# Two graph layers on one core: closings in five spread steps, edge-sum blocks begun one selection later, and the MLP's first layer for 512 nodes inside the last attention pass

## The chip, the cores and the metric

The kernel runs on one core of a Trainium2 chip. The metric is the device time of one launch in microseconds (us), as the median of several runs; the time before is 2317.66 us (three runs, 2315.4 to 2319.2). All profiles are of one execution each.

## The reference, cut to what matters

There are 3327 nodes of 1024 features and a sparse, weighted, symmetric adjacency matrix. Layer 0 is a quantised graph convolution. Layer 1, which the change is about, is graph attention with 8 heads of 64 features, and an MLP behind it:

```python
h = relu(layernorm(x))
Wh = einsum('nf,hfd->hnd', h, W)
e_src = einsum('hnd,hd->hn', Wh, a1)
e_dst = einsum('hnd,hd->hn', Wh, a2)
e = leaky_relu(e_src[:, :, None] + e_dst[:, None, :], 0.2)
e = where(adj[None] > 0, e, -9e15)
att = softmax(e, axis=-1)
enc = elu(einsum('hnm,hmd->hnd', att, Wh)).transpose(1, 0, 2).reshape(n, 512)
out = relu(enc @ W1.T + b1)        # 512 -> 256
out = relu(out @ W2.T + b2)        # 256 -> 256
out = relu(out @ W3.T + b3)        # 256 -> 512
x = x + out @ W4.T + b4            # 512 -> 1024
```

## The kernel before, in words

Nodes are padded to 26 tiles of 128 (`T = 26`). Layer 0 ends with the features, the scores and the mask of the adjacency matrix in DRAM. The change is in what follows, and in one line on the order in which the buffers of layer 0 are laid out.

**Attention as selections.** The exponential of a leaky rectifier has two branches: exp(s + d) if s + d > 0, and exp(0.2 (s + d)) if not. Each factors into a part of the source and a part of the destination. So a head needs, for each node, the sum over neighbours of `f` on the first branch and on the second. The kernel makes a 0/1 *selection* on VectorE (L617): neighbour, and s > -d. TensorE multiplies it with the features (L626, `acc<-sel,f`), with columns for both branches, each split into two parts, 260 columns in all. The second branch's sum over the selected neighbours is then subtracted from its sum over all neighbours. That last sum doesn't depend on the selection; it is the *edge sum* (L534, `mps<-dw,mf`), a product of the mask, cast to floats by ScalarE (L533), with the second branch's features of two heads.

**Passes and units.** The 26 tiles of target nodes fall in two halves of 13, and each half in 7 + 6 tiles. A *pass* is one head for 7 or 6 target tiles: 26 selections of 7 x 128 or 6 x 128 elements, each followed by 7 or 6 matmuls. A *unit* is four passes: two heads, one half. There are 8 units and 32 passes, 832 selections. The loop over passes is `for i, (c, g, e, si) in enumerate(attends)`; in the text, n counts selections from 0 to 831, and j within a pass. Selections have four buffers (pool `sel`), accumulators seven PSUM banks.

**Edge sums between the selections.** A unit has 13 edge blocks of 26 matmuls. The generator `all_edges` yields after each matmul, and `edge_steps(n)` says how many are to be done by selection n: unit 0's until n = LATE, then each later unit's within 104 selections. In the first six selections of a unit's span none are due, in the next 13 two each. A block accumulates in the only bank of the pool `s3_m`. At its end ScalarE copies the bank to `part` (L538), and after 7 and 13 blocks VectorE adds the two parts into `md` (L542).

**Closing.** After a pass ScalarE copies the accumulators to `xs` (L638), VectorE adds the parts (L641, `su`), and `close` does the rest: ScalarE scales the first branch (L567), VectorE subtracts and adds (L568, L569) and takes the reciprocal of the denominator (L571), ScalarE normalises and forms the exponential (L574 to L577), VectorE finishes (L579), and GpSimd's queue writes the result to `enc_d` (L580). For a pass with `e == 0` the closing is issued at selection 24 of the next pass, for one with `e == 1` at the end of its own pass.

**MLP.** Seven groups of 4 tiles (the last of 2). Each group is transposed (L719), goes through three layers (`dense`, L683, with the rectification on ScalarE at L690) and the output layer (L731), is added to `x1` and the bias on VectorE (L727, L741) and written out. Loads are issued on SP (L698, L700 for nodes; L669 for weights).

The order on each engine is made by a scheduler from the program; an instruction given to `tc.keep_in_program_order` stays where the program has it.

Of the kernel before, what the change touches and what calls it, by code (L numbers as in the profile page):

```python
# [8 lines left out]
F32 = mybir.dt.float32  # L9
# [50 lines left out]
def two_layer_kernel(  # L60
# [103 lines left out]
    def large(stack, name, shape, dtype=F32):  # L164
        pool = tc.tile_pool(name=name, bufs=1, side="right", reuse_waits="tile")
        return stack.enter_context(pool).tile(shape, dtype, name=name)

    with tc.tile_pool(name="wh", bufs=1, reuse_waits="tile") as whp, tc.tile_pool(
# [57 lines left out]
        with tc.tile_pool(name="s1", bufs=2, reuse_waits="tile") as s1, tc.tile_pool(  # L226
# [94 lines left out]
            w_life.close()  # L321
            supp = ExitStack()

            s_int = [large(supp, f"s_int{t}", [P, F], F32R) for t in range(T)]

            whead = whp.tile([P, KF, EMB], F32, name="whead")
            a1_t = whp.tile([P, EMB], F32, name="a1_t")
# [144 lines left out]
    STEPS = 4 * T  # L472
    EDGE = 13 * T
    START = T - 2
    LATE = 2 * T + START
    with ExitStack() as wide, tc.tile_pool(name="f1", bufs=1, reuse_waits="tile") as f1p, tc.tile_pool(
        name="sel", bufs=4, reuse_waits="tile"
    ) as selp, tc.tile_pool(name="srow", bufs=2, reuse_waits="tile") as srowp, tc.tile_pool(name="mf", bufs=2, reuse_waits="tile") as mfp, tc.tile_pool(
        name="md", bufs=2, reuse_waits="tile"
# [1 line left out]
        name="s3_acc", bufs=7, space=PSUM, reuse_waits="tile"  # L481
    ) as acc_ps, tc.tile_pool(name="s3_m", bufs=1, space=PSUM, reuse_waits="tile") as m_ps:
        f_odd = f1p.tile([P, T, HW], F32R, name="f_odd")
        masks = [large(wide, "mask0", [P, 7, T, P], U8)]
        f_even = large(wide, "f_even", [P, T, HW], F32R)
        dw = large(wide, "dw", [P, T, HW], F32R)
        masks.append(large(wide, "mask1", [P, 6, T, P], U8))
        xs = large(wide, "xs", [P, 7, 2, 2 * HC])

        def load_features(dst, ap, h, pieces):  # L490
            for js in pieces:
# [17 lines left out]
        def all_edges():  # L509

            for u, (c, g) in enumerate(units):
# [13 lines left out]
                for i in range(len(blocks)):  # L525
                    mask = upcoming
                    if i + 1 < len(blocks):
                        upcoming = mask_of(i + 1)
                    ps = m_ps.tile([P, HW], F32, tag="mps", name="mps")
                    for j in range(T):  # L530
                        if j % TH == 0:
                            mf = mfp.tile([P, TH, P], F32R, tag="mf", name="mf")
                            nc.scalar.copy(mf, mask[:, j : j + TH, :])  # L533
                        nc.tensor.matmul(ps, mf[:, j % TH, :], dw[:, j, :], start=(j == 0), stop=(j == T - 1))  # L534
                        if j == T - 1:
                            if i in (0, 7):
                                part = mdp.tile([P, 7, 2, 2 * HC], F32, tag="part", name="part", bufs=1)
                            nc.scalar.copy(part[:, i % 7], ps.rearrange("p (q c) -> p q c", q=2))  # L538
                            if i in (6, 12):
                                r = slice(i - i % 7, i + 1)  # L540
                                n = i % 7 + 1
                                nc.vector.tensor_tensor(md[:, r], part[:, :n, 0], part[:, :n, 1], ALU.add)  # L542
                        yield

        def edge_steps(n):

            if n < START:
                return min(n, START)
            if n < LATE:
                return START + (EDGE - START) * (n - START) // (LATE - START)  # L550
            u, m = divmod(n - LATE, STEPS)
            if u == len(units) - 1:
                return EDGE * len(units)

            first = min(T, max(0, (m - 6) * 2))
            return EDGE * (u + 1) + first + (EDGE - T) * max(0, m - 19) // (STEPS - 19)

        mds = []
        late = None
        edges = all_edges()  # L560
        done = 0
        def close(h, sub, su, md):

            nb = len(sub)
            up, dn = su[:, :nb, 0], su[:, :nb, 1]
            for b, t in enumerate(sub):
                nc.scalar.activation(up[:, b], up[:, b], AF.Copy, scale=ratio[:, t, h : h + 1])  # L567
            nc.vector.tensor_tensor(dn, md, dn, ALU.subtract)  # L568
            nc.vector.tensor_tensor(up, up, dn, ALU.add)  # L569
            rs = small.tile([P, 7, 1], F32, tag="rs", name="rs")  # L570
            nc.vector.reciprocal(rs[:, :nb], up[:, :, HD:])  # L571
            ht = s3.tile([P, 7, HD], F32, tag="ht3", name="ht3", bufs=2)
            for b in range(nb):
                nc.scalar.activation(ht[:, b], up[:, b, :HD], AF.Copy, scale=rs[:, b])  # L574
            ex = s3.tile([P, 7, HD], F32, tag="ex", name="ex")
            nc.scalar.activation(ex[:, :nb], ht[:, :nb], AF.Relu, scale=-1.0)
            nc.scalar.activation(ex[:, :nb], ex[:, :nb], AF.Exp, scale=-1.0)  # L577

            nc.vector.scalar_tensor_tensor(ht[:, :nb], ex[:, :nb], -1.0, ht[:, :nb], ALU.add, ALU.max)  # L579
            nc.gpsimd.dma_start(  # L580
                enc_d[sub[0] * P : (sub[-1] + 1) * P, h * HD : (h + 1) * HD].rearrange(
                    "(b p) d -> p b d", p=P
                ),
                ht[:, :nb],
            )

        old, young = PARTS[:3], [range(20, 24), range(24, 25), range(25, 26)]
        load_mask(0, SUBS[0])
# [6 lines left out]
            load_features(dw, dsum_d, 0, [js])  # L595
        load_features(f_odd, feat_d, 1, old + young)
        for i, (c, g, e, si) in enumerate(attends):
            h = 2 * g + e
            sub, mask = halves[c][si], masks[si]
            nb = len(sub)  # L600
# [3 lines left out]
            for j in range(T):  # L604
# [24 lines left out]
                while done < edge_steps(n + 1):  # L629
                    next(edges)  # L630
                    done += 1
                if j == START and late is not None:
                    late()
                    late = None
            srow = srow_next
            md = mds[i // 4][:, sub[0] - 13 * c : sub[0] - 13 * c + nb, e * HC : (e + 1) * HC]
            for b in range(nb):
                nc.scalar.copy(xs[:, b], accs[b].rearrange("p (q c) -> p q c", q=2))  # L638
            su = s3.tile([P, 7, 2, HC], F32, tag="su", name="su")
            s2d = su.rearrange("p b q c -> p b (q c)")  # L640
            nc.vector.tensor_tensor(s2d[:, :nb], xs[:, :nb, 0], xs[:, :nb, 1], ALU.add)  # L641
            late = lambda h=h, sub=sub, su=su, md=md: close(h, sub, su, md)
            if e == 1:
                late()
                late = None

    mlp = ctx.enter_context(ExitStack())
    row = large(mlp, "row", [P, 7 * NP // 4])  # L650
    enc_x1 = [large(mlp, "nodes0", [P, T * HW])]
    weights = large(mlp, "weights", [P, T * HW])
    enc_x1.append(large(mlp, "nodes1", [P, 4 * (EMB + F)]))
    enc_x1 = [
        (
            n[:, : 4 * EMB].rearrange("p (q e) -> p q e", q=4),
            n[:, 4 * EMB : 4 * (EMB + F)].rearrange("p (q e) -> p q e", q=4),
        )
        for n in enc_x1
    ]  # L660
    bb4 = row[:, :F]
    bb1, bb2, bb3 = (row[:, F + 4 * i : F + 4 * i + 4] for i in range(3))
    w_at = 0

    def weight(ap, k, m):
        nonlocal w_at
        wt = weights[:, w_at : w_at + k * m].rearrange("p (k m) -> p k m", k=k)
        w_at += k * m
        nc.sync.dma_start(wt, ap.rearrange("(k p) m -> p k m", p=P))  # L669
        return wt  # L670

    w1, w2, w3 = weight(w1t, EMB // P, D1), weight(w2t, D1 // P, D2), weight(w3t, D2 // P, D3)
    with tc.tile_pool(name="s4", bufs=2, reuse_waits="tile") as s4, tc.tile_pool(
        name="s4_ps", bufs=4, space=PSUM, reuse_waits="tile"
    ) as ps_p, tc.tile_pool(name="s4_o", bufs=2, space=PSUM, reuse_waits="tile") as o_ps:

        def dense(xt, k_n, wt, bt, m_n, cols, tag):

# [13 lines left out]
                )  # L692
            return yt

        def load_nodes(i, t0):
            enc, x1 = enc_x1[i]
            for q, t in enumerate(range(t0, min(t0 + 4, T))):
                nc.sync.dma_start(enc[:, q, :], enc_d[t * P : (t + 1) * P, :])  # L698
            for q, t in enumerate(range(t0, min(t0 + 4, T))):
                nc.sync.dma_start(x1[:, q, :], x1_d[t * P : (t + 1) * P, :])  # L700

        load_nodes(0, 0)
        w4 = weight(w4t, D3 // P, F)
        nc.sync.dma_start(bb4, b4.partition_broadcast(P))
        with nc.allow_non_contiguous_dma(reason="biases of a few hundred elements"):
            for bb, b in ((bb1, b1), (bb2, b2), (bb3, b3)):
                m = b.shape[0] // P
                nc.sync.dma_start(bb[:, :m], b.rearrange("(m p) -> p m", p=P))
        for g, t0 in enumerate(range(0, T, 4)):
            tiles = range(t0, min(t0 + 4, T))  # L710
            cols = len(tiles) * P
            enc, x1 = enc_x1[g % 2]
            if t0 + 4 < T:
                load_nodes((g + 1) % 2, t0 + 4)
            enct = s4.tile([P, EMB // P, 512], F32, name="enct")
            for k in range(EMB // P):
                tp = ps_p.tile([P, 512], F32, tag="ps", name="tp4")
                for q, t in enumerate(tiles):
                    nc.tensor.transpose(  # L719
                        tp[:, q * P : (q + 1) * P], enc[:, q, k * P : (k + 1) * P], ident  # L720
                    )
                nc.scalar.copy(enct[:, k, :cols], tp[:, :cols])
            h1 = dense(enct, EMB // P, w1, bb1, D1 // P, cols, "h1")
            h2 = dense(h1, D1 // P, w2, bb2, D2 // P, cols, "h2")
            h3 = dense(h2, D2 // P, w3, bb3, D3 // P, cols, "h3")
            for q, t in enumerate(tiles):
# [60 lines left out]
```

## Time and profile before

| what | before |
|---|---|
| median of three runs | 2317.66 us |
| the profiled execution's own time | 2316.48 us |
| its span, first to last instruction | 2314.7 us |
| mean granted TensorE clock | 0.995 |
| first attention matmul to the last one | 988.5 to 2003.3 us |
| MLP, first transpose to the end | 2003.8 to 2314.7 us |

The engines are TensorE (PE, with its weight loads as PEld), VectorE (DVE), ScalarE (ACT), GpSimd (POOL) and SyncE (SP, which only issues transfers). A line of the timeline holds the start, the length, the engine, the line of the kernel, the operation and its tiles; in brackets stands how long the engine was idle just before, and what it then waited for. A line of the waits holds the total in us, how many times, and the longest. [...]

### The profile page before, as it was taken

What the parts mean: (1) busy time and instruction counts of PE and PEld (TensorE: products, weight loads), DVE (VectorE), ACT (ScalarE), POOL (GpSimd) and SP (SyncE); (2) the same over time, 40 slices, a digit from 0 to 9 for tenths busy, and PEclk for the clock granted to TensorE, in tenths of its full rate; (3) what the DMA queues carried; (4) which work ended last, traced back from release to release, by engine and by line L of the source; (5) the groups of instructions that cost most, each with busy time, mean ns of one, the idle gap of its engine ahead of it and who ended that gap; (6) DMA issues with size and microseconds to landing.
All of it is one profiled execution on the core that took longest, in us unless ns stands there. A gap on an engine that the chain in (4) does not pass through costs nothing. (4 is left out here: it accounts for less than half of the span.)

```text
span 2314.7 us, 32013 instructions
## 1 busy us (share of the span) xinstructions
PE 2252.5 (97%) x12884; PEld 1788.4 (77%) x12896; DVE 1567.1 (68%) x2090; ACT 1003.0 (43%) x1654; POOL 119.0 (5%) x173
## 2 busy tenths in 40 slices
PE   4999999999999999899999999999999999999999
PEld 2467777777777777589999999999999999644444
DVE  7845555555555555487999999999999999812211
ACT  4743334333333333346555555555555555311110
POOL 0000011011110110100000000000000000000000
PEclk9999999999999999999999999999999999999999
DMA  6324444444444444743324241545242332433311
GB/s 231 128 90 149 147 159 135 154 157 149 152 152 137 165 155 144 278 145 112 112 73 147 80 146 45 197 156 162 79 143 83 117 105 71 152 109 114 131 56 55
DMA packets 150302, 304.94 MB, mean 132 GB/s; under 512 B 10173, under 2 KB 91021, under 8 KB 150153
## 3 DMA queue, kind: packets, MB, share of 16 engines
q1 hardware_dynamic: 130248, 229.72, 29.7%
q0 software_dynamic: 19904, 73.17, 9.7%
q8 instruction: 101, 1.65, 0.3%
q14 instruction: 49, 0.39, 0.1%
HBM read 216.07 MB, written 86.79 MB: 131 GB/s over the span
## 5 line engine op out<-in xcount | busy, mean ns | idle before, releaser
L617 DVE SCALAR_TENSOR_TENSOR sel<-srow,ndst,mask 128x896 fp32r<-128x896 f32 (+1 forms) x832 | 869.6, 1082 | 61.2 <-PE acc L626 49.7
L534 PE MATMUL mps<-dw,mf 128*128 128x260 f32 x2704 | 462.7, 284 | 0.0
L443 PE MATMUL mm<-s_int,hi 128*128 128x512 f32 x1352 | 433.0, 399 | 0.0
L443 PE MATMUL mm<-s_int,lo 128*128 128x512 f32 x1352 | 421.6, 391 | 0.0
L626 PE MATMUL acc<-f_even,sel 128*128 128x260 f32 x2704 | 403.9, 284 | 1.4 <-DVE sel L617 1.3
L533 ACT CAST mf<-mask 128x1664 fp32r<-128x1664 uint8 x208 | 330.0, 1588 | 167.1 <-PE mps L534 129.3
L626 PE MATMUL acc<-f_odd,sel 128*128 128x260 f32 x2704 | 393.9, 285 | 6.9 <-DVE sel L617 6.8
L534 PEld LDWEIGHTS mps<-dw,mf 128*128 128x128 f32 x2704 | 379.8, 188 | 9.3 <-ACT part L538 8.4
L626 PEld LDWEIGHTS acc<-f_odd,sel 128*128 128x128 f32 x2704 | 352.6, 188 | 15.9 <-DVE sel L617 12.2
L626 PEld LDWEIGHTS acc<-f_even,sel 128*128 128x128 f32 x2704 | 356.7, 188 | 5.9 <-DVE sel L617 2.8
L443 PEld LDWEIGHTS mm<-s_int,lo 128*128 128x128 f32 x1352 | 253.8, 188 | 57.6 <-issue 5.7
L443 PEld LDWEIGHTS mm<-s_int,hi 128*128 128x128 f32 x1352 | 252.1, 188 | 55.6 <-issue 5.7
L184 DVE TENSOR_SCALAR mk<-at 128x896 uint8<-128x896 f32 x104 | 61.7, 593 | 262.6 <-DMA at<-in_adj_t 261.9
L179 ACT CAST hi<-at 128x896 fp32r<-128x896 f32 x104 | 92.7, 891 | 328.7 <-PE mm L443 294.8
L384 PE MATMUL whm<-whead,ht 128*128 128x512 f32 x416 | 186.9, 602 | 0.8 <-ACT ht L381 0.8
L731 PE MATMUL o<-weights,h 128*128 128x512 f32 x416 | 179.7, 592 | 0.0
L731 PEld LDWEIGHTS o<-weights,h 128*128 128x128 f32 x416 | 79.0, 190 | 99.1 <-issue 99.0
L384 PEld LDWEIGHTS whm<-whead,ht 128*128 128x128 f32 x416 | 77.5, 191 | 98.1 <-issue 87.7
L183 DVE TENSOR_TENSOR lo<-at,hi 128x896 fp32r<-128x896 f32 x104 | 106.6, 1025 | 51.3 <-ACT hi L179 39.9
L538 ACT COPY part<-mps 128x260 f32<-128x260 f32 x104 | 39.1, 376 | 216.3 <-PE mps L534 216.3
L741 DVE TENSOR_TENSOR yo<-o,nodes 128x1024 f32<-128x1024 f32 (+1 forms) x27 | 31.8, 1182 | 146.0 <-PE o L731 146.0
L332 PE MATMUL mm<-w_int,xqt 128*128 128x512 bf16 x404 | 98.3, 393 | 9.5 <-DVE w_int L319 7.3
(128 smaller groups left out, 1566.9 us busy)
## 6 DMA issues: line engine op xcount, KB each, us to landing
feat_d<-fw POOLq DMA_DIRECT2D x26, 1040.0 KB, 5.3
f_even<-feat_d SPq DMA_DIRECT2D x7, 3380.0 KB, 12.8
f_odd<-feat_d SPq DMA_DIRECT2D x7, 3380.0 KB, 13.6
at<-in_adj_t SPq DMA_DIRECT2D x52, 448.0 KB, 3.9
at<-in_adj_t SPq DMA_DIRECT2D x52, 384.0 KB, 3.1
mask<-mask_d SPq DMA_DIRECT2D x39, 416.0 KB, 7.7
dw<-dsum_d SPq DMA_DIRECT2D x16, 910.0 KB, 5.1
dsum_d<-dw POOLq DMA_DIRECT2D x26, 520.0 KB, 6.5
```

The lines of the kernel that those rows point to most:

```text
L179: ins = nc.scalar.copy(hi, at)
L183: nc.vector.tensor_tensor(lo, at, hi.bitcast(F32), ALU.subtract)
L184: nc.vector.tensor_scalar(mk[:, r], at, 0.0, None, ALU.is_gt)
L332: nc.tensor.matmul(mm[:, c * 512 : (c + 1) * 512], xqts[t][:, k, :], w_int[:, k, c * 512 : (c + 1) * 512], start=(k == 0), stop=(k == KF - 1),
L384: nc.tensor.matmul(whm, ht[:, k, :], whead[:, k, :], start=(k == 0), stop=(k == KF - 1))
L443: nc.tensor.matmul(mm[:, c * 512 : (c + 1) * 512], which[:, q, :], s_int[j][:, c * 512 : (c + 1) * 512], start=(j == 0 and which is hi), s ...
L533: nc.scalar.copy(mf, mask[:, j : j + TH, :])
L534: nc.tensor.matmul(ps, mf[:, j % TH, :], dw[:, j, :], start=(j == 0), stop=(j == T - 1))
L538: nc.scalar.copy(part[:, i % 7], ps.rearrange("p (q c) -> p q c", q=2))
L617: nc.vector.scalar_tensor_tensor(sel[:, :nb], srow[:, :nb], ndst[:, j, h : h + 1], mask[:, :, j, :], ALU.is_gt, ALU.mult,)
L626: nc.tensor.matmul(accs[b], sel[:, b, :], f[:, j, :], start=(j == 0), stop=(j == T - 1))
L731: nc.tensor.matmul(ps[:, c * 512 : (c + 1) * 512], h3[:, k, q * P : (q + 1) * P], w4[:, k, c * 512 : (c + 1) * 512], start=(k == 0), stop= ...
```

## The change

Four things, and what they need.

- **Closings.** `close` becomes a generator of five steps. Its VectorE instructions are kept in program order. At every third selection (every second, if two closings are open) one step is issued, if the edge sums that the next step needs are done.
- **Edge blocks.** After the last matmul of a block the loop stops until the next selection. `LATE` becomes 62 instead of 76, and the last unit's edges are spread over 118 selections instead of 104.
- **First layer.** Transposes and first layer of the MLP for the first 512 nodes are issued within the last pass, through the bank of the edge sums, one step at selections 6 to 9 and then at each second one. The MLP's buffers lie in those of the features, the edge features and the first mask, which are given up before the last pass.
- **Layout.** Buffers on the right side are laid out in another order, and the buffers of layer 0 in reverse, so that the same ones overlap.

```diff
-            s_int = [large(supp, f"s_int{t}", [P, F], F32R) for t in range(T)]
+            s_int = [large(supp, f"s_int{t}", [P, F], F32R) for t in reversed(range(T))][::-1]
...
-    LATE = 2 * T + START
+    LATE = 62
+    LAST = 14
+    xs = large(wide, "xs", [P, 7, 2, 2 * HC])
+    masks = [None, large(wide, "mask1", [P, 6, T, P], U8)]
+    dw = large(early, "dw", [P, T, HW], F32R)
+    f_even = large(early, "f_even", [P, T, HW], F32R)
+    masks[0] = large(early, "mask0", [P, 7, T, P], U8)
...
-            u, m = divmod(n - LATE, STEPS)
-            if u == len(units) - 1:
-                return EDGE * len(units)
+            u = min((n - LATE) // STEPS, len(units) - 2)
+            m = n - LATE - STEPS * u
+            span = STEPS + (LAST if u == len(units) - 2 else 0)
             first = min(T, max(0, (m - 6) * 2))
-            return EDGE * (u + 1) + first + (EDGE - T) * max(0, m - 19) // (STEPS - 19)
+            rest = (EDGE - T) * max(0, m - 19) // (span - 19)
+            return EDGE * (u + 1) + first + min(rest, EDGE - T)
...
-        def close(h, sub, su, md):
+        def close(i):
...
+            sums = EDGE * (i // 4) + (EDGE if si else 7 * T)
+            yield 0
+            su = s3.tile([P, 7, 2, HC], F32, tag="su", name="su")
+            pin(nc.vector.tensor_tensor(s2d[:, :nb], xs[:, :nb, 0], xs[:, :nb, 1], ALU.add))
             for b, t in enumerate(sub):
                 nc.scalar.activation(up[:, b], up[:, b], AF.Copy, scale=ratio[:, t, h : h + 1])
-            nc.vector.tensor_tensor(dn, md, dn, ALU.subtract)
-            nc.vector.tensor_tensor(up, up, dn, ALU.add)
+            yield sums
+            pin(nc.vector.tensor_tensor(dn, md, dn, ALU.subtract))
+            yield 0
+            pin(nc.vector.tensor_tensor(up, up, dn, ALU.add))
+            yield 0
-            nc.vector.reciprocal(rs[:, :nb], up[:, :, HD:])
+            pin(nc.vector.reciprocal(rs[:, :nb], up[:, :, HD:]))
...
+            yield 0
+            pin(nc.vector.scalar_tensor_tensor(ht[:, :nb], ex[:, :nb], -1.0, ht[:, :nb], ALU.add, ALU.max))
...
+        def close_more():
+            if closing and closing[0][1] <= done:
+                gen = closing[0][0]
+                need = next(gen, None)
+                closing[0] = gen, need
+                if need is None:
+                    closing.pop(0)
...
+            if i == len(attends) - 1:
+                early.close()
...
+                load_nodes(0, 0)
+                w1 = weight(w1t, EMB // P, D1)
...
+                def first_layer():
+                    for k in range(EMB // P):
+                        tp = m_ps.tile([P, 512], F32, tag="mps", name="tp0")
+                        for q in range(4):
+                            nc.tensor.transpose(
+                                tp[:, q * P : (q + 1) * P],
+                                enc_x1[0][0][:, q, k * P : (k + 1) * P],
+                                ident,
+                            )
+                        nc.scalar.copy(enct0[:, k], tp)
+                        yield
+                    for m in range(D1 // P):
+                        ps = m_ps.tile([P, 512], F32, tag="mps", name="h0_ps")
+                        for k in range(EMB // P):
+                            nc.tensor.matmul(ps, w1[:, k, m * P : (m + 1) * P], enct0[:, k],
+                                start=(k == 0), stop=(k == EMB // P - 1))
+                            if k == EMB // P - 1:
+                                nc.scalar.activation(h1_0[:, m], ps, AF.Relu, bias=bb1[:, m : m + 1])
+                            yield
...
                 while done < edge_steps(n + 1):
                     next(edges)
                     done += 1
-                if j == START and late is not None:
-                    late()
-                    late = None
+                    if done % T == 0:
+                        break
+                if i == len(attends) - 1 and FRONT <= j and (j < FRONT + 4 or j % 2 == 0):
+                    next(first_group, None)
+                pace = 2 if len(closing) > 1 else 3
+                if j % pace == pace - 1:
+                    close_more()
...
-            late = lambda h=h, sub=sub, su=su, md=md: close(h, sub, su, md)
-            if e == 1:
-                late()
-                late = None
+            gen = close(i)
+            closing.append((gen, next(gen)))
+        while closing:
+            close_more()
...
+        enc_x1.append(nodes("nodes1"))
...
+            if g == 0:
+                h1 = h1_0
```

## The prediction

> **What bounds the kernel now.** First the page's busy line, then busy time by stretch (one full unit of attention, the last pass, the MLP):
>
> ```profile
> PE 2252.5 (97%) x12884; PEld 1788.4 (77%) x12896; DVE 1567.1 (68%) x2090; ACT 1003.0 (43%) x1654; POOL 119.0 (5%) x173
> core 0: us, PE busy (x) PEld busy (x) DVE busy (x) ACT busy (x) POOL busy (x), PEclk, DMA share, GB/s
> 1235.00:1360.00 125.00, 124.49 (x1012) 122.25 (x1011) 119.12 (x127) 68.59 (x124) 3.64 (x4) 1.00 0.33 105
> 1990.00:2006.00 16.00, 14.91 (x99) 12.46 (x99) 15.99 (x18) 2.68 (x8) 0.97 (x1) 1.00 0.06 15
> 2006.00:2315.00 309.00, 303.11 (x788) 140.46 (x786) 61.72 (x55) 53.09 (x97) 0.85 (x1) 0.99 0.29 101
> ```
>
> TensorE bounds nearly everything; only the last pass belongs to VectorE (15.99 of 16.00). A unit (one pair of heads, one half of the nodes) is 4 passes = 104 selections: 104 x 6.5 attention matmuls + 13 x 26 edge matmuls = 1014. How long is one? Within runs the timeline spaces starts by 0.120 us: attention runs start at 1300.32 and 1301.40 with 6 + 3 matmuls between, 1.08 / 9. So 1014 x 0.120 = 121.7 us is the floor. The unit's real period is 125.5 us: TensorE's longest wait for a selection recurs at 1107.61 and, two units on, at 1358.68. So 3.8 us per unit are lost. Where? Idle before the weight loads in the same unit, then one edge block's end, then that long wait:
>
> ```profile
> PEld mps L534 <- ACT part L538: 1.0, 5, 0.2
> PEld acc L626 <- DVE sel L617: 0.9, 2, 0.7
> PEld acc L626 <- ACT xs L638: 0.2, 1, 0.2
> ...
> 1302.12 0.52 PE L534 MATMUL mps<-dw,mf 128*128 128x260 f32 x3
> 1302.47 0.64 PE L626 MATMUL acc<-f_even,sel 128*128 128x260 f32 x4
> 1302.67 0.38 ACT L538 COPY part<-mps 128x260 f32<-128x260 f32 x1 [2.08 <-PE mps L534]
> 1303.10 0.19 PEld L534 LDWEIGHTS mps<-dw,mf 128*128 128x128 f32 x1 [0.20 <-ACT part L538]
> 1303.10 0.39 PE L534 MATMUL mps<-dw,mf 128*128 128x260 f32 x1
> ...
> 1358.68 0.99 PE L626 MATMUL acc<-f_odd,sel 128*128 128x260 f32 x6 [0.48 <-DVE sel L617]
> ```
>
> An edge block's last matmul starts at 1302.36; the next block can start 0.74 us later, after the copy out of the only bank. Four attention matmuls lie between: 5 x 0.12 = 0.60. So 0.14 is lost, and as the weights were not loaded ahead, the next start comes 0.105 later than usual: 0.25 per block end. A unit has five of these and a 0.2: 1.45 us. Waits for a selection (at 1357.2 and 1358.7, with refills) cost 1.05; the handing over of banks at pass ends some 0.75; the rest is scattered.
>
> VectorE's slack, and the end of attention:
>
> ```profile
> DVE sel L617 <- PE acc L626: 4.5, 24, 0.3
> DVE su L641 <- ACT xs L638: 0.5, 2, 0.4
> ...
> 1990.42 12.16 DVE L617 SCALAR_TENSOR_TENSOR sel<-srow,ndst,mask 128x768 fp32r<-128x768 f32 x13
> ...
> 2006.25 7.30 PE L683 MATMUL h_ps<-enct,weights 128*128 128x512 f32 x16
> 2013.39 10.84 PE L683 MATMUL h_ps<-h,weights 128*128 128x512 f32 x24
> 2024.06 10.46 PE L731 MATMUL o<-weights,h 128*128 128x512 f32 x24
> ```
>
> Back to back a 6-block selection costs 12.16 / 13 = 0.935 us (alone it shows 1.02), a 7-block one about 1.06. Embedded small operations cost less than they show too: start to next start 0.48 to 0.55 for the 0.56 to 0.64 us adds, 0.11 for the reciprocal. VectorE's floor per unit is 52 x (0.935 + 1.06) + 10.4 for four closings + 1.9 for the edge sums = 116 us.
>
> **Which measure of headroom.** By TensorE's busy row, 124.49 of 125, nothing is left: 0.5 us per unit, 4 in all. The Trainium skill (Perfetto Trace Analysis, Identifying the Most-Contended Engine) says that matmul busy time is no measure of headroom and the weight loads' share is: 122.25 of 125, so 2.75 per unit, 22 in all, near my spacing. The same section takes occupancy as fair for VectorE, and that speaks against this change: 119.1 of 125 leaves 5.9 us, and the pinned waits below would use it up, for a gain of nothing here. The back-to-back spacing says 116 and 9.5 us of slack. I take the trace's spacing.
>
> **The change, part by part.** Against the profiled execution: span 2314.7, time 2316.48, 1.2 below the median.
>
> *Edge blocks one selection later.* In the built order, six or seven attention matmuls now lie between every two blocks: the next start comes 7 x 0.12 = 0.84 or 0.96 us on, against 0.74 needed. Cover is thin with six (0.10), so I leave 0.2 of the 1.45: gain 1.25 per unit. If ScalarE is in a 1.59 us mask cast when a block ends, up to 1.6 comes back, once; the built order puts the copies ahead of the next casts.
>
> *Closings spread, their VectorE steps pinned.* Operations and durations are the same; where two closings stood together within 7 selections at the end of a unit (568, 569, 571, 641, 579, 568, 569, 571: 3.8 us in six selections), now one step follows every third selection. The stretch short of edge matmuls after a unit's last block is now five 7-block selections plus about 11 with one to six edge matmuls each. There VectorE needs 16 x 1.06 + 2.4 (edge sum and four steps) = 19.4 us, TensorE 16 x 0.84 + 27 x 0.12 = 16.7; four buffers give a lead of some 2.5. The wait falls from 1.05 to 0.3: gain 0.75 per unit.
>
> *New waits.* The first add of a closing stands after 3 or 4 selections of the new pass and waits for six or seven accumulator copies (0.25 to 0.3 each, about 1.8 us after the pass's last matmul). A full four-selection lead makes VectorE wait 0.8 (after 4) or 2 (after 3); before it waited 0.5 per unit. Queued behind are the selections, and TensorE behind those. The last step stands 4 selections (4.3 us at least) after the reciprocal; its ScalarE chain is 1.78 + 0.58 + 0.58 = 3.0, or 4.6 with a cast between. Bounds: 0 and 3.6 us per closing; nearest to the 0.4 and 0.2 us waits shown, but with a fuller lead, I take 1.4, or 5.6 per unit. 116 + 5.6 = 121.6, under TensorE's new 123.5: hidden.
>
> *LATE 62 for 76.* Unit 0's 314 edge matmuls fall on 38 selections rather than 52, the last unit's on 14 more; TensorE's sum stays. In the last unit TensorE has 118 x 0.78 + 338 x 0.12 = 132.6 us, VectorE 116 x 118 / 104 = 131.6: cost 0, up to 4 if the waits show there. The edge features' loads (first piece issued 1340.61, landed 4.8 later) move along on SP; the piece is free over 6 us before the block ends and needed five selections after it. At the change of halves seven mask loads move past the per-block ones: 0, at most 5 us once.
>
> *Reversed buffers.* The same memory comes free in the same order: 0.
>
> Attention: 2.0 x 8 units = 16 us.
>
> *First layer in the last pass.* Before: 16 transposes (1.75) and 8 matmuls (each recorded as two: 17.54 / 20 = 0.877 each, 7.0) after the last pass. In it TensorE has 156 x 0.12 = 18.7 us of work in about 29, so 8.75 more fits; but late matmuls crowd: the last 8 selections give VectorE 8.1 us and TensorE 8 x 0.72 + 4 x 0.877 = 9.3, so the pass ends 1.2 later. Its loads go early on SP as before (nodes landed 1945.85 to 1954.79; first weights 5.3 us after their issue).
>
> What is late next: the last closing. In the built order four 1.22 us bias adds stand before its first add on VectorE, and its 6 scalings (1.55) and 6 normalisings (1.54) stand on ScalarE each before a rectification (0.69) of the second layer. From the last attention matmul's end T: adds done about T+3, first add T+4, scalings T+5.6, rectification T+6.3, normalisings, second rectification T+8.6; seven of the third layer's eight matmuls follow: T+14.7. Before, that point was 2024.06 with T = 2003.5; now 2003.5 + 1.2 + 14.7 = 2019.4: gain 4.7 us, not 8.75. Without the queueing 8.3; with double 1.
>
> The second group's node loads now wait for the last closing's write, about 10 us later than 2005.87; the first output add is queued behind them on VectorE, but TensorE has two output banks, 13.7 us: hidden by some 8.
>
> Sum: 16 + 4.7 = 20.7. 2316.5 - 20.7 = 2295.8; against the median, 2297.
>
> **Rivals.** (1) VectorE becomes the bound through its pinned waits: a unit stays at 125, attention gains 0 to 5, the tail 5: 2308 to 2313. For: the lead grows as TensorE stalls less. Against: 9.5 us of slack. (2) Slower: the same waits at their upper end, 3.6 us in each closing: 116 + 14.4 = 130.4 per unit, 8 x 4.9 - 4.7 = +34, 2352. It decides from 2.5 us per closing. (3) Only bank handovers and scatter stay (unit 122.4) and the tail's rectifications are not queued: 25 + 8 = 33, 2285. (4) The first layer does not hide, the last pass grows by what is saved: 16 alone, 2302.
>
> **Numbers.** Forecast with (4): 0.70; (3) 0.12; (1) 0.11; (2) 0.07. The forecast's own range is 2290 to 2304; 2286 to 2309 leaves out two in ten, half of (3), most of (1) and (2). What a measurement can tell from no change is about 0.2%, 4.6 us: faster 0.88 (some of (1) falls within), same 0.05, slower 0.07.
>
> **What would show it.** Unit period 123.5 (125.5 before); waits of edge weight loads for the part copy near 0 (8.4 us over attention); waits of VectorE's first closing add for the accumulator copies up, from 3.6 to 20 to 40 us; TensorE idle before the third layer's second matmul by 2 to 4 us; output matmuls of group 0 starting about 15 us after the last attention matmul. Wrong if TensorE's waits for selections exceed 15 us over attention, or the last pass grows by over 3.

## The result, and the profile after

The changed kernel takes 2293.2 us in the median (2292.1 to 2294.8, 4 runs), the kernel before 2317.9 beside it. The ratio is 0.9895, 95% interval 0.9878 to 0.9912. The forecast was 2297.0 within 2286 to 2309. The profiled execution spans 2291.7 us, against 2314.7.

The busy line of the page, then busy time by stretch: one full unit (123 us now) and the last pass. The columns are TensorE, weight loads, VectorE, ScalarE, GpSimd.

```profile
PE 2233.5 (97%) x12896; PEld 1785.0 (78%) x12896; DVE 1559.1 (68%) x2090; ACT 998.2 (44%) x1654; POOL 119.3 (5%) x173
1235.00:1358.00 123.00, 123.00 (x1014) 122.37 (x1013) 118.53 (x127) 68.42 (x125) 3.64 (x4) 1.00 0.34 106
1959.00:1989.00 30.00, 29.32 (x196) 24.51 (x194) 29.98 (x37) 12.24 (x37) 1.81 (x2) 1.00 0.54 181
```

The busy line hardly differs; the stretches do. TensorE's 1014 matmuls of a unit now fill 123.00 of 123.00 us. In the last pass TensorE and VectorE are both nearly full, where before VectorE alone was:

```profile
1976.00:2004.00 28.00, 24.50 (x161) 20.55 (x160) 28.00 (x36) 9.95 (x35) 1.81 (x2) 1.00 0.41 138
```

The waits over the whole of attention, before and then after: TensorE, its weight loads, VectorE.

```profile
PE acc L626 <- DVE sel L617: 8.0, 13, 2.0
PEld acc L626 <- DVE sel L617: 15.0, 36, 2.2
PEld mps L534 <- ACT part L538: 8.4, 43, 0.2
DVE sel L617 <- PE acc L626: 49.7, 208, 0.7
DVE su L641 <- ACT xs L638: 3.6, 14, 0.4
```

```profile
PE acc L738 <- DVE sel L729: 1.1, 1, 1.1
PEld acc L738 <- DVE sel L729: 4.3, 16, 1.3
PEld mps L539 <- ACT part L543: 0.3, 1, 0.3
DVE sel L729 <- PE acc L738: 41.2, 142, 1.7
DVE su L580 <- ACT xs L753: 2.8, 8, 0.4
```

The copy out of the edge bank stops one weight load instead of 43, and selections hold up the weight loads less than a third as long. The last row is the one that the prediction wanted at 20 to 40: it fell.

By the starts of the attention matmuls, where the span's 23.0 us went:

| | before | after | gain, us |
|---|---|---|---|
| first attention matmul | 988.5 | 989.4 | -0.9 |
| attention without its last pass | 987.6 | 970.3 | 17.3 |
| last pass, first to last matmul | 27.2 | 29.2 | -2.0 |
| last attention matmul to first output matmul | 20.7 | 12.1 | 8.6 |

The later start can't be put down to the change: in the eleven kernels here that leave attention's start alone it lies between 986.1 and 990.5.

The unit's period fell from 125.53 to 123.20 us. A matmul of 260 columns is recorded with 0.28 us, but the next one starts 0.120 us after it. Summing over a unit what each start lies beyond that spacing gives 3.84 us lost before, 1.52 now. Sorted by place and by what the weight load waited for, as the mean of units 2 to 6:

| lost per unit, us | before | after |
|---|---|---|
| block ends (part copy) | 1.42 | 0 |
| selections, later in a pass | 1.23 | 0.40 |
| first 2.5 us of a pass (accumulator banks) | 1.12 | 1.10 |
| rest | 0.07 | 0.04 |

The tail, from the timeline of after, by engine (TensorE, VectorE, ScalarE; in brackets the idle time before and its releaser):

```profile
1987.92 1.28 PE L738 MATMUL acc<-f_odd,sel 128*128 128x260 f32 x6
1989.80 3.70 PE L772 MATMUL h_ps<-rest,weights 128*128 128x512 f32 x8 [0.60 <-ACT xs L753]
1994.08 7.13 PE L772 MATMUL h_ps<-h,weights 128*128 128x512 f32 x16 [0.57 <-ACT h L779]
2001.05 17.33 PE L809 MATMUL o<-weights,h 128*128 128x512 f32 x40
...
1985.23 1.01 DVE L729 SCALAR_TENSOR_TENSOR sel<-srow,ndst,mask 128x768 fp32r<-128x768 f32 x1
1986.15 4.63 DVE L805 TENSOR_TENSOR nodes<-nodes,rest 128x1024 f32<-128x1024 f32 x4
1990.90 0.97 DVE L580 TENSOR_TENSOR su<-xs 128x780 f32<-128x780 f32 x1
...
1991.90 1.55 ACT L583 ACTIVATE su<-su,ratio 128x65 f32<-128x65 f32 x6 [1.04 <-DVE su L580]
1993.36 0.67 ACT L779 ACTIVATE h<-h_ps,rest 128x512 f32<-128x512 f32 x1
1994.36 1.54 ACT L593 ACTIVATE ht<-su,rs 128x64 f32<-128x64 f32 x6 [0.34 <-ACT h L779]
1995.81 0.67 ACT L779 ACTIVATE h<-h_ps,rest 128x512 f32<-128x512 f32 x1
```

The last attention matmul starts at 1988.92, so T (its end, in the prediction's sense) is 1989.1. The four bias adds begin 3 us ahead of T and end at 1990.8. The second rectification is late (1995.81 to 1996.48), but the third layer's 16 records run through without a gap, 0.43 us from start to start. The weight load that waits for the second rectification is that of the seventh record:

```profile
1996.52 0.42 PEld L772 LDWEIGHTS h_ps<-h,weights 128*128 128x128 f32 x2 [0.43 <-ACT h L779]
```

Its matmul, the fourth of eight (two records each), starts on the beat at 1996.76. The chain that ended last shows what set the end:

```profile
1992.49 0.96 ACT su L583 x4
1993.45 0.58 ACT h L779
1994.03 0.04 issue
1994.08 7.13 PE h_ps L772 x16
2001.21 27.47 PE o L809 x64
```

One queueing, of the last scalings ahead of the first rectification, is on the chain. The normalisings are not.

### The profile page after: what moved, and what is told of

Its sections match the earlier page's. It is cut to its first block, busy times and chain, and to the rows that moved or that the text cites. A ratio compares the mean times of both kernels' runs of the same rounds, so it can differ in the third digit from the quotient of the medians.

```text
span 2291.7 us, 32041 instructions
## 1 busy us (share of the span) xinstructions
PE 2233.5 (97%) x12896; PEld 1785.0 (78%) x12896; DVE 1559.1 (68%) x2090; ACT 998.2 (44%) x1654; POOL 119.3 (5%) x173
## 3 DMA queue, kind: packets, MB, share of 16 engines
q8 instruction: 101, 1.65, 0.3%
## 5 line engine op out<-in xcount | busy, mean ns | idle before, releaser
L539 PE MATMUL mps<-dw,mf 128*128 128x260 f32 x2704 | 453.3, 283 | 0.1
L738 PE MATMUL acc<-f_even,sel 128*128 128x260 f32 x2704 | 396.9, 284 | 1.4 <-DVE sel L729 1.1
L538 ACT CAST mf<-mask 128x1664 fp32r<-128x1664 uint8 x208 | 331.3, 1593 | 123.5 <-PE mps L539 100.2
L333 PE MATMUL mm<-w_int,xqt 128*128 128x512 bf16 x416 | 97.7, 386 | 10.2 <-DVE w_int L319 7.7
```

The lines of the kernel that those rows point to most:

```text
L333: nc.tensor.matmul(mm[:, c * 512 : (c + 1) * 512], xqts[t][:, k, :], w_int[:, k, c * 512 : (c + 1) * 512], start=(k == 0), stop=(k == KF - 1),
L738: nc.tensor.matmul(accs[b], sel[:, b, :], f[:, j, :], start=(j == 0), stop=(j == T - 1))
```

## Experiments

Each ratio is to the kernel before, run on the same chip in the same batch; after stands at 0.9895. A point of the ratio's third place is 2.3 us. Differences to after are those of the medians; in 8 to 10 and 12, where the kernel before ran up to 2 us faster or slower beside the two, they go by the ratios. "Lost per unit" is the sum beyond the 0.120 us spacing in units 2 to 6: 3.84 before, 1.52 after.

**1. Without the later edge blocks.** The rest of the change stays.

```diff
                     done += 1
-                    if done % T == 0:
-                        break
```

> The changed kernel with one line pair taken out: an edge block may begin at once behind the block before it. In the built order six blocks per unit then begin four attention matmuls after the last matmul of the block before, as in the kernel before. Theory (the bank's handover costs 0.25 us at each such block end): the unit goes from 123.2 to 124.5-124.7 us, waits of edge weight loads for the part copy return to about 8 us over attention, the whole gets slower by 10-12 us than the changed kernel: about 2304. Rival (these stalls lie beside VectorE's waits, and the spread closings are what frees the unit): less than 3 us, below 2297.

Measured: 2303.66 us, 0.9945 [0.9932, 0.9959], 10.5 above after (11.6 by the ratios). Lost per unit 2.69, 1.16 more, and the wait returns:

```profile
PEld mps L539 <- ACT part L543: 9.7, 50, 0.2
```

**2. Only the later edge blocks, in the kernel before.**

```diff
                     next(edges)
                     done += 1
+                    if done % T == 0:
+                        break
```

> The kernel before with one thing added: edge-sum blocks begin one selection later. Closings, LATE and the first layer as before. Theory (block ends are lost TensorE time whatever else is done; 1.25 us per unit): 10 us under before, about 2307. Rival (without the spread closings VectorE cannot follow a faster TensorE, and the stall moves into waits for selections): at most 5 us under, 2312 or more.

Measured: 2305.54 against 2315.78 beside it, 0.9953 [0.9940, 0.9965]: 10.2 us. Lost per unit falls by 1.37 to 2.47. So the blocks are worth about 10 us with and without the rest. The same waits, in this kernel's lines:

```profile
PE acc L626 <- DVE sel L617: 7.7, 13, 2.0
PEld acc L626 <- DVE sel L617: 14.3, 34, 2.2
```

They stayed where they were (8.0 and 15.0): the stall did not move over to the selections.

**3. Closings as before (not spread, not pinned), with LATE 76 and LAST 0 as before.** The later blocks and the moved layer stay.

```diff
-    LATE = 62
-    LAST = 14
+    LATE = 76
+    LAST = 0
...
-                pace = 2 if len(closing) > 1 else 3
-                if j % pace == pace - 1:
-                    close_more()
+                if j == START:
+                    while closing:
...
+                        close_more()
...
+            close_more()
+            while e == 1 and closing:
...
+                close_more()
```

> The changed kernel with the closings as before (all at once, at selection 24 of the next pass or at the end of the own pass, not pinned) and LATE 76, LAST 0, so that they stand where they stood; the break between edge blocks and the first layer in the last pass stay. Theory (bunched closings starve TensorE once per unit, spreading frees 0.75 us per unit): 5-8 us slower than the changed kernel, about 2300, with one wait of TensorE for a selection of 0.5 us or more per unit. Rival (the break alone does it): within 2 us of the changed kernel.

Measured: 2300.81, 0.9929 [0.9916, 0.9941], 7.6 above after. Lost per unit 2.43, and one wait for a selection per unit is back (0.51 us in the unit from 1373):

```profile
PE acc L738 <- DVE sel L729: 6.2, 9, 1.5
```

The edit holds two things, so each was run alone.

**4. LATE 76 and LAST 0 alone.**

> The changed kernel with LATE 76 and LAST 0: the edge sums of every unit 14 selections later, all else as changed. Theory (TensorE's sum is the same, the early LATE only places the stretch poor in edge matmuls): within 3 us of the changed kernel, either way. Rival (the spread closings need the early sums, or the poor stretch then meets 6-block passes and closings held up): TensorE's waits for selections grow by 0.5-1 us per unit, 4-8 us slower.

Measured: 2296.63, 0.9910 [0.9896, 0.9923], 3.4 above after; lost per unit 1.93. The median lies between the two expectations and the interval overlaps after's, so the unit decides: its period is 123.61 against 123.20. That is the rival's direction, and less than its 0.5 to 1. Selections hold up the attention weight loads more often:

```profile
PEld acc L738 <- DVE sel L729: 6.4, 27, 1.3
```

**5. Closings as before, LATE kept at 62.** The edit of 3 without its first part.

> The kernel after with the closings placed and ordered as before, but LATE kept at 62 (the earlier run with the old closings had LATE 76 too). It splits that run's 7.6 us and the 3.4 us of LATE alone. Theory (the two burdens lie at the same place, the end of a unit, and do not add: with the old closings LATE decides less than alone): 5 to 7 us over after, 2298 to 2300. Rival (the closings' place alone is worth the prediction's 0.75 us per unit less nothing, LATE adds to it): 3 to 4.5 us over, 2296 to 2297.5.

Measured: 2298.99 against 2318.07, 0.9919 [0.9906, 0.9933]; lost per unit 2.15; 5.8 above after, within the theory's range. Over after, per unit: LATE alone 0.4, closings alone 0.6, both 0.9. The two add up nearly, so the theory's reason, that they should not add, was wrong.

**6. Steps given out late but not pinned.**

```diff
         def pin(ins):
-            tc.keep_in_program_order(ins)
+            return ins
```

> The kernel after with the closings still given out in five steps, but their VectorE steps free to be placed by the scheduler and not pinned. Theory (the spread needs the pin, since unpinned steps are drawn to where their inputs come ready, in bursts): 2 to 5 us over after, 2295 to 2298. Rival (giving the steps out late is enough): within 1.5 us, 2292 to 2295.

Measured: 2294.22 against 2318.07, 0.9899 [0.9885, 0.9912], lost per unit 1.53: no difference. VectorE's order in the two traces says why: in all of attention only one reciprocal and one last step of a closing stand a selection earlier. The rival held, but the run can't tell what pinning would be worth where a scheduler wanted otherwise.

**7. The first layer after the last pass, as before.** The call within the loop goes, and group 0 computes its first layer with the other groups' code.

```diff
-                if i == len(attends) - 1 and FRONT <= j and (j < FRONT + 4 or j % 2 == 0):
-                    next(first_group, None)
...
-            if g == 0:
-                h1 = h1_0
-            else:
+            if True:
```

> The changed kernel with the first group's transposes and first layer back after the last pass (its loads, the closings and the blocks as changed). Theory: the last pass gets shorter by 2 us, from 29.4 to 27.3, and the stretch from the last attention matmul to the first output matmul longer by 8.4, from 12.3 to 20.7: 6-7 us slower than the changed kernel, about 2300. Rival (the first layer takes as much from the last pass as it saves): no difference.

Measured: 2300.92, 0.9928 [0.9916, 0.9941], 7.7 above after. Its last pass takes 27.3 us, so the layer lengthens it by 2.0. From its last attention matmul at 1987.8 to the output matmuls it is again 20.7 (12.1 in after):

```profile
1990.70 7.29 PE L770 MATMUL h_ps<-enct,weights 128*128 128x512 f32 x16
1997.83 10.84 PE L770 MATMUL h_ps<-h,weights 128*128 128x512 f32 x24
2008.50 10.03 PE L805 MATMUL o<-weights,h 128*128 128x512 f32 x23
```

**8 and 9. VectorE's slack.** In after, the first add and the last step of each closing are issued twice (8), or three times (9); the repeats write the same values.

```diff
             pin(nc.vector.tensor_tensor(s2d[:, :nb], xs[:, :nb, 0], xs[:, :nb, 1], ALU.add))
+            pin(nc.vector.tensor_tensor(s2d[:, :nb], xs[:, :nb, 0], xs[:, :nb, 1], ALU.add))
...
             pin(nc.vector.scalar_tensor_tensor(ht[:, :nb], ex[:, :nb], -1.0, ht[:, :nb], ALU.add, ALU.max))
+            pin(nc.vector.scalar_tensor_tensor(ht[:, :nb], ex[:, :nb], -1.0, ht[:, :nb], ALU.add, ALU.max))
```

> The kernel after with the first add and the last step of every closing issued twice (the second writes the same values): 1.46 us more on VectorE per closing, 5.85 per unit. It measures VectorE's slack. Theory (floor 116 us per unit by back-to-back spacing, waits of the pinned steps near nothing as in the trace of after, so 7.2 us of 123.2 are free): 0 to 8 us over after, 2293 to 2301. Rival A (the prediction's 5.6 us of waits per unit are there, hidden): 121.6 + 5.85 = 127.5 per unit, some 34 us over, 2327. Rival B (occupancy is the measure, 118.5 of 123 in the stretch of one unit): 124.4 per unit, 9 us over, 2302.

> The same with both steps issued three times: 11.7 us more on VectorE per unit. Theory: 116 + 11.7 = 127.7 per unit, 4.5 over 123.2, so about 36 us over after, 2329. Rival A (5.6 us of waits besides): 133.3 per unit, 80 us over, 2373. Rival B (occupancy): 130.2 per unit, 56 us over, 2349.

Measured: 2295.61, 0.9912 [0.9898, 0.9925] for twice; 2335.95, 1.0084 [1.0070, 1.0098] for three times (2315.78 beside both). Twice costs 3.9 us by the ratios, and 0.4 per unit (period 123.60): 5.85 us more work is nearly free, where waits of 5.6 would have made it 4.3 per unit and occupancy 1.2. Three times costs 44 us, nearest to the 36 of the theory. Units 2 to 7 lose 7.4 us each, 5.9 over after; so VectorE's floor is at most 123.2 + 5.9 - 11.7 = 117.4. Part of that may not be VectorE's: in each of these six units TensorE now waits once for edge features, whose loads land late.

```profile
PE mps L539 <- DMA dw<-dsum_d: 12.7, 6, 2.9
```

That is 2.1 in each; if all of it adds to the period, the floor is 115.3. The prediction's 116 lies between. No run separates the two, but VectorE idles only 1.5 us per unit there. The same stretch of the twofold kernel, then of the threefold:

```profile
1235.00:1358.00 123.00, 123.00 (x1012) 122.13 (x1011) 121.81 (x134) 68.92 (x125) 3.65 (x4) 1.00 0.34 106
```

```profile
1235.00:1358.00 123.00, 119.07 (x967) 117.20 (x967) 121.80 (x137) 65.78 (x120) 3.64 (x4) 1.00 0.33 105
```

VectorE's busy time is the same, 121.8 of 123, in a kernel where it hardly costs and in one where it sets the pace. Only TensorE's count (x1012, x967) tells them apart.

**10. The first selections held.** Not foreseen: in after the first four selections of attention stand, on VectorE, ahead of the last two tiles' layer-norm and score work, and wait there for a load. The row names that of the edge features, which a selection doesn't read; that of the source scores (`srow`), which it does read, landed at 969.72. VectorE's timeline, then TensorE's longest waits up to attention's first matmuls, both of after:

```profile
970.12 1.15 DVE L729 SCALAR_TENSOR_TENSOR sel<-srow,ndst,mask 128x896 fp32r<-128x896 f32 x1 [7.63 <-DMA dw<-dsum_d]
```

```profile
PE sp L399 <- DVE src L393: 12.1, 2, 9.9
```

```diff
-                nc.vector.tensor_scalar(ndst[:, t], dst, -1.0, None, ALU.mult)
+                ins = nc.vector.tensor_scalar(ndst[:, t], dst, -1.0, None, ALU.mult)
+                if t == T - 2:
+                    held.append(ins.ins)
...
+                with tc.issue_after(held[0]) if i == 0 and j < 8 else nullcontext():
                     nc.vector.scalar_tensor_tensor(sel[:, :nb], ...)
```

> The kernel after, with the first eight selections of pass 0 held on VectorE behind the negation of the destination scores of the last tile but one. They stood ahead of the last two tiles' layer-norm and score work and waited 7.6 us there for a load, while TensorE waited 9.9 us for VectorE. Theory: 5 to 8 us under after, 2285 to 2288. Rival (the selections are what attention's start waits for in any case, so holding them only moves the wait): 2292 to 2295.

Measured: 2285.36 against 2315.78, 0.9868 [0.9855, 0.9882], about 6 us under after: faster than both kernels. Of TensorE's waits for the score work only two of 2.2 us are left, and attention starts at 980.0, not 989.4:

```profile
PE sp L401 <- DVE src L393: 4.4, 2, 2.2
```

**11. The same hold in the kernel before.**

> The kernel before with the first eight selections held behind the negation of the destination scores of the last tile but one. Theory (the wait in front of attention is there in before too, 5.9 us of VectorE and 10.3 us of TensorE, and is apart from this change): 4 to 6 us under before. Rival (only the later edge blocks make the first selections stand in the way): within 1 us of before.

Measured: 2311.03 against 2318.07, 0.9970 [0.9958, 0.9982], 7.0 us: a little over the theory. Attention starts at 983.0 instead of 988.5. The wait was in before too and is apart from the change.

**12. The hold, and LATE at 48.**

> The kernel with the held first selections, and LATE at 48: unit 0's edge matmuls end 14 selections earlier and every later unit's begin 14 earlier, so the last pass keeps fewer of them. Theory (LATE is worth about 0.4 us per unit from 76 to 62 because fewer edge blocks meet the closings, and that goes on; the last pass, full on TensorE and on VectorE in after, gets shorter by 1 to 2): 1 to 5 us under the run with held selections alone, 2280 to 2285. Rival (what counts is where blocks lie against pass ends, and at 62 they lie well by chance): 1 to 4 us over it, 2286 to 2290.

Measured: 2291.78 against 2317.99, 0.9886 [0.9870, 0.9903]: worse than 10 by about 4. The theory missed, and the time lies above the rival's range too. Full units take 123.30 us, 0.1 more than at 62. The last pass does get 0.9 shorter (28.3), but attention as a whole gets 4.9 longer (1004.3 for 999.5), and about 3 of it is lost in the last unit. Attention also starts 2.8 later than in 10, which is within the spread of its start. Busy time in the last unit, here and then in 10:

```profile
1868.20:1987.20 119.00, 117.82 (x906) 110.76 (x904) 116.12 (x126) 51.49 (x112) 3.62 (x4) 1.00 0.35 113
1858.30:1979.50 121.20, 120.53 (x950) 115.30 (x948) 118.76 (x128) 56.74 (x118) 3.62 (x4) 1.00 0.34 113
```

With 872 matmuls of attention and edges and 8.75 us for the MLP's first layer, TensorE needs 872 x 0.12 + 8.75 = 113.4 of 119.0 us; in 10 it is 916 x 0.12 + 8.75 = 118.7 of 121.2. VectorE is busy for 116.1 of the 119.0. Edge matmuls that end earlier leave TensorE without work there, while unit 0 grows by them. From 76 to 62 LATE gained, from 62 to 48 it lost; of the three, 62 is best, so LATE is a balance and not a direction.

**Not run alone: the layout.** The three parts, each taken away (1, 3 and 7), cost 10.5, 7.6 and 7.7: 25.8 us, for 24.7 in all. That leaves nothing beyond the noise for the order of the buffers, as predicted, but it is not shown by a run.

## Why the prediction was right, and where not

- **Edge blocks.** Predicted 1.25 us per unit; 1.16 lost without them in after, 1.37 gained by them in before, and the wait for the part copy gone in both. The mechanism (0.74 us needed, 0.84 or 0.96 given) holds.
- **Closings spread.** Predicted 0.75 per unit, with LATE 62 at no cost and no gain. Closings and LATE together give 0.9: closings 0.5 to 0.6, LATE 0.3 to 0.4, by which is changed first. The sum was nearly right by the wrong shares. LATE was looked at in unit 0 and in the last, but not in the units between, where it also shifts blocks against the closings. What it removes there is, by the traces of 4 and after, mostly waits for selections (0.71 to 0.40 us per unit), and 0.10 at block ends.
- **The unit.** 123.20 for 123.5; rival (3) had 122.4. Of the 1.52 us still lost, 1.10 lies at the starts of passes, where banks are handed over. The prediction put that at 0.75 in before, where the trace has 1.12; it makes no difference to the sum, as nothing was to be gained there.
- **New waits.** The term of 5.6 us per unit, 1.4 per closing, was mis-sized: VectorE waits for the accumulator copies 2.8 us in all of attention, 0.35 per unit. The step that failed is "a full four-selection lead makes VectorE wait 0.8 (after 4) or 2 (after 3)". After four selections the lead was full in two closings of each unit, and the wait was 0.35 and 0.06. One of them, in after and at the same place in before:

```profile
1409.00 2.05 ACT L753 COPY xs<-acc 128x260 f32<-128x260 f32 x7
1409.72 1.02 DVE L729 SCALAR_TENSOR_TENSOR sel<-srow,ndst,mask 128x768 fp32r<-128x768 f32 x1 [0.29 <-PE acc L738]
1411.08 1.11 DVE L580 TENSOR_TENSOR su<-xs 128x910 f32<-128x910 f32 x1 [0.35 <-ACT xs L753]
...
1409.74 1.02 DVE L617 SCALAR_TENSOR_TENSOR sel<-srow,ndst,mask 128x768 fp32r<-128x768 f32 x1 [0.17 <-PE acc L626]
1411.11 1.11 DVE L641 TENSOR_TENSOR su<-xs 128x910 f32<-128x910 f32 x1 [0.35 <-ACT xs L638]
```

In after the old pass's last matmul starts at 1409.40. The fourth selection waits for the buffer which that matmul frees, starts 0.32 us later and ends 1.34 us after it. The copies have begun before it and end 1.65 after it; 0.3 remains, not 0.8. In before the fourth selection waited for its buffer too, so the 0.4 us wait that the prediction saw was already that of a full lead. After three selections, once per unit, the lead was short: at 1472 VectorE was one selection ahead, the copies ended before its third selection did, and it did not wait where 2 us had been put. In the fourth closing VectorE was 0.4 us short of a full lead and did not wait either. Experiment 8 excludes hidden waits of 5.6 us: they would have shown as 34 us. So rivals (1) and (2) fall. Experiment 9 shows that VectorE as the bound is real from some 6 to 7 us per unit on.
- **Occupancy against spacing.** The Trainium skill (Perfetto Trace Analysis, Identifying the Most-Contended Engine) takes VectorE's occupancy as fair. It would have given 1.2 us per unit in experiment 8 and 56 us in 9. The measured 0.4 lies within the spacing's 0 to 1; the measured 44 lies between 36 and 56, a little nearer to 36. The choice of the trace's spacing was right.
- **Last pass.** Predicted 1.2 longer, measured 2.0 by experiment 7. That term counted only the crowd in the last eight selections. Up to the eleventh TensorE starts on a selection some 0.1 us after VectorE has made it. From the twelfth on it falls behind: by 0.8 at the nineteenth and by 1.7 at the last, which VectorE ended at 1986.24 and TensorE began at 1987.92. So some 0.6 of the delay was there before the last eight. In experiment 7 it stays under 0.1 us to the end.
- **Tail.** Predicted T+14.7 to the output matmuls, measured T+11.9. Two steps failed. "Adds done about T+3": they were done at T+1.7, as VectorE began them 3 us ahead of T. "Second rectification T+8.6; seven of the third layer's eight matmuls follow": the first three need only the first half of the sum, so five follow, and the late rectification (T+7.4 for T+8.6) is just covered. TensorE idles 0.57 before the layer's first matmul and not before its second. Tail and layer gain 6.6 net of the longer pass, for 4.7; rival (4), no gain, falls by experiment 7.
- **The sum.** 17.3 for 16 in attention and 6.6 for 4.7 in the tail, less 0.9 of a later start (within its spread), make the span's 23.0, for 20.7. The medians differ by 24.7; the other 1.7 is the spread of single runs. So the forecast lay 3.8 us high, inside its range: it was too cautious on the tail and the unit, too hopeful on the last pass. That the term of the closings came out so near is in part luck: LATE gave what the closings did not.

## What to carry to other kernels

Find each small wait's own count and refill by the spacing of matmul starts, and price an edit by them: 0.25 us times five block ends times eight units was the whole gain of 10 us. What a wait on an in-order queue costs is the difference of two chains: when the queue gets there, and when what it waits for is done. Count both from the same event in a timeline, and see whether the wait shown there is already one of a full lead. And before tuning a loop that is 99% full, look at how it begins: four selections queued too early cost 6 us, a quarter of what the whole change brought.

## What was not expected of the hardware

VectorE's busy row stops telling near its end: 121.81 and 121.80 of 123.00 us, at unit periods of 123.6 and about 129. Its instructions overlap when queued back to back (0.935 us apart, 1.02 shown), so a row can show less room than there is: that of after, 118.53 of 123.00, held 5.85 us of further work for 0.4 us.
